# A four-layer image kernel: the order of the first loads and sums, and the last chunk and tail of a scan

## Chip, cores and metric

The kernel runs on one core of a Trainium2 chip. The metric is the device time in microseconds of one execution; before the change the median of three runs is 3623.33 us.

## What is computed

An input of 48 x 48 positions with 768 channels, float32, goes through four layers: an attention block, a spectral filter, a scan with a rotating state, and a second spectral filter. Two places of it matter here. The attention block begins with a layer norm and one product:

```python
xn = layernorm(x, ln1_g, ln1_b)
qkv = xn.reshape(B, H * W, C) @ qkv_w + qkv_b
```

The scan layer makes its inputs from one projection of x, then applies twelve steps and an output product:

```python
B_proj = silu(x @ W_B + b_B + B_bias)      # C_proj the same; Xb = silu(x @ W_X + b_X)
alpha = jax.nn.sigmoid(x @ W_dec + b_dec)  # gamma the same, from W_lam
theta = x @ W_th + b_th
for i in range(12):
    inj = _rope(B_base, theta * (i + 1)) * Xb
    Hst = diffuse(Hst)                     # a 3 x 3 convolution of each channel
    Hst = alpha * Hst + inj                # i = 0
    Hst = alpha * Hst + (1.0 - gamma) * alpha * prev + gamma * inj   # i > 0
    prev = inj
Hg = _rope(C_base, theta * 12) * Hst
return silu(Ho @ W_out + b_out)            # Ho is Hg with its axes turned
```

## The kernel before

Large products are done as 2 x 2 block products with seven terms instead of eight. So each needs sums of blocks of both operands, made on VectorE or GpSimd. The tile framework orders each engine's instructions by its own planner; an instruction pinned with `keep_in_program_order` keeps its place in the order of the program.

**Start of the attention block** (`qkv_phase`). Rows of x come in tiles of 128 x 768, three to a block, loaded on SP's queue by `load_x` (line 282), behind the loads of ln_g and ln_b (line 109). `prepare` normalises three tiles: statistics, a square root on ScalarE and small operations on VectorE (lines 73 to 88), scaling (line 89), then transposes on TensorE into PSUM (line 98) and evacuation with gain and bias, in turn on ScalarE and VectorE (lines 100, 102). The transposes use the pool `qkv_t` with two banks; the products of v use `qkv_m` with six. The weights of the first column block come as w[0], w[1], w[6] and a21 (lines 411 to 415). `combine` makes w[3], w[2], w[5], w[4] of them on GpSimd (lines 134 to 137). `sums` makes the same kind of sums of x on VectorE (lines 142 to 145), named t1, t2 and t4 here; the second of them overwrites a block of x. `rows_in_seven` (line 156) then runs the seven products of v in groups of nine matmuls, called v_0 to v_6. v_2 needs w[2] and t2. Partial results of v_0 are copied by ScalarE (line 172), those of v_1 and later added by VectorE (lines 174 to 180), and GpSimd adds the bias (line 299).

On SP's queue the store of all seven blocks of w to DRAM (line 431, 4 MB) stands early, ahead of most loads for the products of q and k (lines 348 to 350). The sums of those weights are GpSimd's too. `load_windows` (line 194) loads a table of relative positions on ScalarE's queue at the very start and copies it on VectorE; rm is its maximum (line 425), kb the scaled bias of k (line 423).

**Projection for the scan** (`scan_phase`). The projection (line 1186) runs in eight chunks q. After each, VectorE adds biases into za and g (line 1187), the angle is reduced (lines 1081 to 1087), ScalarE makes its sines (lines 1161, 1162), the SiLUs (line 1203) and the sigmoids (lines 1206, 1207); VectorE turns B (line 1380) and makes H (line 1216) and the states s0 and s1 (lines 1244 to 1250). In the last chunk several are pinned. Changing between groups of functions on ScalarE shows in the trace as a load of a table. ScalarE also spreads alpha (line 1263) and multiplies by gamma (line 1226).

**The scan** has eleven steps of eight groups of channels. TensorE does the convolution (line 1279) into four PSUM tiles of two banks, VectorE multiplies by alpha and adds the state (lines 1281, 1283), GpSimd prepares the next product t (line 1287), a tile of a ring of six, which ScalarE copies into PSUM (line 1288). GpSimd also turns C between steps, with c and cr tiles of the same ring (line 1380), and stores it to cr_d.

**The tail.** In the last step a group of turned C is loaded back as crg, two buffers (line 1291), and multiplied with H into the tile s0, by GpSimd for seven groups and by VectorE for the eighth (line 1305). When the scan's pools are closed, `turned` transposes the result on TensorE (line 1348) and ScalarE copies it into tiles hT of a new pool (line 1350), whose memory is that of the closed pools. The output products (line 1364), called so, follow, and with them the first products of the last layer, so_f (line 1495).

Of the kernel before, what the change touches and what calls it, by code (L numbers as in the profile page):

```python
# [12 lines left out]
F32 = mybir.dt.float32  # L13
# [7 lines left out]
P = 128  # L21
G = 48
# [16 lines left out]
NWR = KP * KTW  # L39
NBR = NWR + KP * 2 * KTH  # L40
SAFE = 64.0

NB, BS = 8, 96
KW = G // 2 + 1
# [48 lines left out]
def transpose_norm(nc, psum, xhs, xnT, ident, g, b, name):  # L93

    for cc in range(NC):
        ps = psum.tile([P, 512], F32, tag="t", name=f"{name}_tp{cc}")
        for t in range(3):
            nc.tensor.transpose(ps[:, t * P : (t + 1) * P], xhs[t][:, cc * P : (cc + 1) * P], ident)
        if cc % 2:
            nc.vector.tensor_scalar(xnT[:, cc, :], ps[:, :TB], g[:, cc : cc + 1], b[:, cc : cc + 1], ALU.mult, ALU.add)  # L100
        else:
            nc.scalar.activation(xnT[:, cc, :], ps[:, :TB], AF.Identity, bias=b[:, cc : cc + 1], scale=g[:, cc : cc + 1])


def load_cols(nc, pool, v, n, name):

    t = pool.tile([P, n], F32, tag=name, name=name)
    with nc.allow_non_contiguous_dma(reason="small vector"):
        nc.sync.dma_start(t, v.rearrange("(n p) -> p n", p=P))
    return t  # L110


# [19 lines left out]
def combine(eng, p, s1, s2, s3, s4):  # L132

    eng.tensor_tensor(s1, p[2], p[3], ALU.add)
    eng.tensor_tensor(s2, s1, p[0], ALU.subtract)
    eng.tensor_tensor(s3, p[0], p[2], ALU.subtract)
    eng.tensor_tensor(s4, p[1], s2, ALU.subtract)
# [56 lines left out]
def load_windows(nc, pool, relT):  # L194


    t = pool.tile([P, 2, 2 * G - 1, 2], F32, tag="windows", name="windows")
    rel = pool.tile([P, 2, 2 * G - 1], F32, tag="rel", name="rel")
    nc.vector.memset(t, 0.0)
    for s in range(2):  # L200
        rows = slice(s * HD, (s + 1) * HD)
        nc.scalar.dma_start(rel[rows], relT)
        nc.vector.tensor_copy(t[rows, :, :, s], rel[rows])
    return t

# [38 lines left out]
        yield  # L244


def qkv_phase(tc, ident, x, qkv_w, qkv_b, windows, ln_g, ln_b, q_d, k_d, v_d, rw_d, rh_d, wqk_d, wv_d, flag, home, ahead):

# [15 lines left out]
    with (  # L266
# [3 lines left out]
        ExitStack() as inner,  # L270
    ):
        kp, xp, wp = (inner.enter_context(tc.tile_pool(name=f"qkv_{n}", bufs=bufs, side="left")) for n, bufs in (("k", 1), ("x", 3), ("w", 3)))
        g = load_cols(nc, kp, ln_g, NC, "ln1_g")
        b = load_cols(nc, kp, ln_b, NC, "ln1_b")
        wv = qkv_w.rearrange("(c p) n -> p c n", p=P)
        Xs, ops = {}, {}

        def load_x(sb, half):
            for t in range(3):
                i = (2 * sb + half) * 3 + t  # L280
                Xs[i] = xp.tile([P, C], F32, tag="x", name=f"x_{i}", bufs=6)
                nc.sync.dma_start(Xs[i], x[i * P : (i + 1) * P, :])

        def prepare(sb, half):

            blk = 2 * sb + half
            if half == 0:
                ops[sb] = home.tile([P, NC * TS], F32, tag="xn", name=f"xnT_{sb}").rearrange("p (c n t) -> p c n t", c=NC, n=2)
            xhs = [layernorm_rows(nc, xp, Xs.pop(3 * blk + t), f"ln1_{blk}_{t}") for t in range(3)]
            transpose_norm(nc, pt, xhs, ops[sb][:, :, half, :], ident, g, b, f"n1_{blk}")  # L290

        def sums(sb):
            ts = (kp.tile([P, NC2, TB], F32, tag=f"x{n}", name=f"xn{n}_{sb}") for n in ("T1", "T2", "T4"))
# [112 lines left out]
        with tc.tile_pool(name="qkv_v0", bufs=1, side="right") as vp:  # L406
            w = vp.tile([P, 7, NC2, TB], F32, tag="wv", name="wv")
            a21 = vp.tile([P, NC2, TB], F32, tag="a21", name="a21")
            load_x(0, 0)
            for k in range(2):  # L410
                nc.sync.dma_start(w[:, k], wv[:, k * NC2 : (k + 1) * NC2, 2 * C : 2 * C + TB])
            prepare(0, 0)
            load_x(0, 1)
            nc.sync.dma_start(w[:, 6], wv[:, NC2:, 2 * C + TB :])
            nc.sync.dma_start(a21, wv[:, :NC2, 2 * C + TB :])
            vb = load_bcast(nc, kp, qkv_b[2 * C : 3 * C], C, "vb")
            qkb = load_cols(nc, kp, qkv_b[0 : 2 * C], 2 * NC, "qkb")
            kb = kp.tile([P, NC], F32, tag="kb", name="kb")
            qms, kms = (qp.tile([P, NC, NSB], F32, tag=n, name=n) for n in ("qms", "kms"))
            prepare(0, 1)  # L420
            combine(nc.gpsimd, (w[:, 0], w[:, 1], a21, w[:, 6]), w[:, 3], w[:, 2], w[:, 5], w[:, 4])
            sums(0)
            V.tensor_scalar(kb, qkb[:, NC : 2 * NC], HD**-0.5, None, ALU.mult)
            rm = qp.tile([P, 2], F32, tag="rm", name="rm")
            V.tensor_reduce(rm, windows.rearrange("p t k s -> p t (k s)"), axis=AX.X, op=ALU.max, apply_absolute_value=True)
            pz = qp.tile([P, 2, NC], F32, tag="pz", name="pz")
            V.memset(pz, 0.0)
            onec = qp.tile([P, 1], F32, tag="onec", name="onec")
            V.memset(onec, 1.0)
            v_rows(0, lambda n: w[:, n])  # L430
            nc.sync.dma_start(wv_d, w)

        with tc.tile_pool(name="qkv_o", bufs=1, side="right") as op:
# [94 lines left out]
            V.tensor_scalar(flag, mx, SAFE, None, ALU.is_lt)  # L528
            while steps or ready:
                advance()  # L530


def load_bias(nc, bt, p0, rw_d, rh_d, h, g, t0, n):
# [352 lines left out]
def mlp_phase(tc, ident, w1s_d, b1, w2, w2s_d, b2, ln_g, ln_b, xr_d, xa_d, follow_in):  # L886
# [8 lines left out]
    with (  # L895
# [18 lines left out]
        def prepare(sb, half):  # L914

            blk = 2 * sb + half
            if half == 0:
                ops[sb] = [cp.tile([P, NC, 2, TB], F32, tag="x2nT", name=f"x2nT_{sb}")]
                ops[sb] += [cp.tile([P, NC2, TB], F32, tag=f"x{n}", name=f"x{n}_{sb}") for n in ("T1", "T2", "T4")]
            xhs = []  # L920
            for t in range(3):
                xt = xp.tile([P, C], F32, tag="x", name=f"ml_x_{blk}_{t}", bufs=6)
                r0 = (3 * blk + t) * P
                nc.sync.dma_start(xt, xr_d[r0 : r0 + P, :])
                xhs.append(layernorm_rows(nc, xp, xt, f"ln2_{blk}_{t}"))
            X, t1, t2, t4 = ops[sb]
            transpose_norm(nc, pt, xhs, X[:, :, half, :], ident, g, b, f"n2_{blk}")
            if half:
                ops[sb] = block_sums(nc, X, t1, t2, t4)

# [162 lines left out]
def scan_phase(tc, ident, w, wts, rows_back, xh, x_close, c_d, cr_d, out_open):  # L1093
# [24 lines left out]
    with tc.tile_pool(name="sc_s", bufs=1, side="left") as sp:  # L1118
# [9 lines left out]
        with (  # L1128
# [15 lines left out]
            with (  # L1144
# [27 lines left out]
                for q in range(NQ):  # L1172
# [3 lines left out]
                    for t in range(R4):  # L1176
# [11 lines left out]
                        biased.pop(0)()  # L1188
                        if t < R4 - 1:
                            biased.pop(0)()  # L1190
                    g3 = g.rearrange("p (n r) t -> p n r t", r=RR)
                    c, x = za[:, :NCR, :], za[:, NA - 1 - RR : NA - 1, :]
                    thz = za[:, NCR + NN : NCR + NN + NM, :]
                    alq = al[:K, :, prs]
                    ga = temp([1, R4], "ga", q)
                    th = temp([NM * R4], "th", q)
                    V.tensor_copy(th, thz.rearrange("p m t -> p (m t)"))
                    cs = sincos(th, q, "t1")

                    pin = tc.keep_in_program_order if q == NQ - 1 else lambda ins: ins  # L1200
                    pin(biased.pop(0)())
                    for t in (x, g, c):
                        pin(nc.scalar.activation(t, t, AF.Silu))

                    V.tensor_tensor(g.rearrange("p (n r) t -> p n (r t)", r=RR), g.rearrange("p (n r) t -> p n (r t)", r=RR), x.rearrange("p r t -> p (r t)").unsqueeze(1).to_broadcast([K, NN, RR * R4]), ALU.mult)
                    pin(nc.scalar.activation(alq, za[:, NCR : NCR + NN, :], AF.Sigmoid))
# [46 lines left out]
            with (  # L1253
# [16 lines left out]
                def step(it, gr):  # L1270
# [13 lines left out]
                    if it + 1 < ITERS:  # L1284
                        t = tp.tile([P, GC, RR, NPR], F32, tag="t", name=f"t_{it}_{gr}")
                        m0 = (gr * GC) % NM
                        GP.tensor_tensor(t, sc[:, ch], c1[:, m0 : m0 + GC].unsqueeze(2).to_broadcast([P, GC, RR, NPR]), ALU.mult)  # L1287
                        nc.scalar.copy(pv, t.rearrange("p (b n) r t -> p b (n r t)", b=2))
                    else:
                        cr = tp.tile([P, NQ, GC * RR, R4], F32, tag="crg", name=f"crg_{gr}", bufs=2)  # L1290
                        nc.sync.dma_start(cr[:K], cr_d[:K, :, gr * GC * RR : (gr + 1) * GC * RR])
                        crs[gr] = cr

# [38 lines left out]
        with (  # L1332
# [7 lines left out]

            yield x3, psum
            hTs = {}

            def turned(j, q4):

                ps = pt.tile([P, 512], F32, tag="t", name=f"ht_{j}_{q4}")
                for t in range(4):
                    nc.tensor.transpose(ps[:, t * P : t * P + K], hg[:K, 4 * q4 + t, j * P : (j + 1) * P], ident[:K, :K])
                hTs[j, q4] = tp.tile([P, 4, 2, G], F32, tag=f"hT{j}_{q4}", name=f"hT_{j}_{q4}", bufs=1)
                nc.scalar.copy(hTs[j, q4], ps.rearrange("p (i s w) -> p i s w", i=4, s=2)[:, :, :, :G])  # L1350


# [31 lines left out]
def block_kernel(ctx: ExitStack, tc: tile.TileContext, a: dict):  # L1384
# [39 lines left out]
            loads[2](bts[g], (0, 0), g)  # L1424
        ahead.extend((loads, kvs, qbs, bts, ones, oneh))

    windows = load_windows(nc, atc, a["relT"])
    qkv_phase(tc, ident, x, a["qkv_w"], a["qkv_b"], windows, a["ln1_g"], a["ln1_b"], q_d, k_d, v_d, rw_d, rh_d, wqk_d, wv_d, flag, home, load_ahead)

    def opened(name, shape, side):  # L1430
        stack = ExitStack()
# [498 lines left out]
```

## Time and profile before

| | |
|---|---|
| runs before | 3623.33, 3620.8, 3623.38 us |
| profiled execution | 3626.7 us, its span 3624.9 us |
| mean granted TensorE clock | 0.987 |
| first TensorE instruction | 11.69 us |
| v_2 begins, TensorE then without a gap to 103 us | 41.25 us |
| last projection product of the scan ends | about 3019.7 us |
| first convolution product | 3030.59 us |
| last convolution product ends | about 3274.7 us |
| transposes resume | 3284.05 us |

All times are from the start of the span. A timeline row has the start, the duration, the engine, the line and the operation, what it writes and reads, and how many instructions are merged; in brackets stands the idle time of the engine before it and what ended it. POOL is GpSimd, DVE VectorE, ACT ScalarE, PE TensorE and PEld its weight loads. A float32 matmul has two records in this trace, a transpose one. Ends of matmuls are modelled.

### The profile page before, as it was taken

Reading aid. Unit: us, or ns where it says so; the run is one execution under the profiler, and the core shown is the slowest. Engines: PE = TensorE matmul, PEld = TensorE weight load, DVE = VectorE, ACT = ScalarE, POOL = GpSimd, SP = SyncE. Lnnn points to the kernel's source line nnn. Section 1 sums busy time; section 2 is a strip of 40 time slices with the busy share of each in tenths; the row PEclk is TensorE's granted clock in tenths of the full one; section 3 lists DMA queues with packets and bytes.
Section 4 is the critical chain, followed back from the end, with each engine's and each line's share of the span. In section 5 each row is a group of like instructions: output and inputs, shape, how many; then the busy total and the mean of one; then the engine's idle time right before and its main releaser. Section 6 shows DMA issues by size and latency. Waiting matters only on the chain.

```text
span 3624.9 us, 52111 instructions
## 1 busy us (share of the span) xinstructions
PE 3539.1 (98%) x20914; PEld 2174.5 (60%) x20914; DVE 2002.9 (55%) x3014; ACT 1138.5 (31%) x1731; POOL 685.8 (19%) x570
## 2 busy tenths in 40 slices
PE   7999999999999999999999999999999998999998
PEld 4666654444444444555555555555578777995685
DVE  6644456767676776564244324233145478994445
ACT  1222244444555554113101210120033365223341
POOL 4211101111111110340000000000023304961131
PEclk9999999999999999999999999999999999999999
DMA  7555555656545443443345334434444303113345
GB/s 248 205 194 173 197 163 164 185 143 157 162 121 151 125 125 86 125 152 125 107 136 174 106 106 140 146 109 123 140 131 105 94 21 104 33 30 101 95 113 157
DMA packets 257371, 477.66 MB, mean 132 GB/s; under 512 B 36031, under 2 KB 209919, under 8 KB 250913
## 3 DMA queue, kind: packets, MB, share of 16 engines
q1 hardware_dynamic: 247152, 453.20, 41.8%
q10 hardware_dynamic: 9968, 21.04, 1.6%
q8 instruction: 168, 2.75, 0.3%
q14 instruction: 83, 0.67, 0.1%
HBM read 330.53 MB, written 143.62 MB: 131 GB/s over the span
## 4 chain that ended last, share of the span: by engine, by line
PE 87%; DVE 4%; DMA 3%; POOL 3%; ACT 2%; issue 1%; SPq 0%; ACTq 0%; DVEq 0%; POOLq 0%
PE p L959 14%; PE p L1022 13%; PE s L623 12%; PE av L654 12%; PE qk L361 6%; PE c L1186 4%; PE v L169 3%; PE s L633 3%; PE pj L169 2%; PE f_z L1594 2%; PE f_z L1595 2%; PE f_x L1559 2%; PE so L1364 2%; PE f_u L1609 2%; POOL t L1287 2%
## 5 line engine op out<-in xcount | busy, mean ns | idle before, releaser
L643 DVE TENSOR_TENSOR acc<-acc,p 128x928 f32<-128x928 f32 (+1 forms) x480 | 560.5, 1168 | 264.1 <-ACT p L635 222.6
L635 ACT ACTIVATE p<-s 128x928 f32<-128x928 f32 (+1 forms) x540 | 505.9, 939 | 492.2 <-PE s L633 470.2
L623 PE MATMUL s<-qt,kv 64*128 64x464 f32 (+1 forms) x2160 | 521.9, 559 | 7.8 <-DMA qt<-q_d 5.7
L1022 PE MATMUL p<-w,h 128*128 128x384 f32 x1512 | 492.7, 486 | 0.0
L654 PE MATMUL av<-p,kv 128*64 128x464 f32 (+1 forms) x2160 | 443.0, 554 | 0.0
L1022 PEld LDWEIGHTS p<-w,h 128*128 128x128 f32 x1512 | 286.2, 190 | 196.9
L633 PE MATMUL s<-bt,oneh 64*128 64x464 f32 (+1 forms) x1080 | 400.9, 731 | 0.7 <-DMA bt<-rh_d 0.7
L654 PEld LDWEIGHTS av<-p,kv 128*64 128x64 f32 x2160 | 147.0, 137 | 262.0 <-issue 250.6
L623 PEld LDWEIGHTS s<-qt,kv 64*128 64x128 f32 x2160 | 203.1, 187 | 164.8 <-issue 153.6
L959 PE MATMUL p<-x2nT,w 128*128 128x384 f32 x864 | 292.7, 488 | 2.8 <-issue 2.8
L1279 PE MATMUL c<-H,bands 128*48 128x96 f32 x5632 | 243.8, 247 | 11.2 <-issue 10.9
L361 PE MATMUL qk<-xnT,wqk 128*128 128x384 f32 x756 | 249.8, 487 | 0.3 <-DMA wqk<-wqk_d 0.3
L1279 PEld LDWEIGHTS c<-H,bands 128*48 128x48 f32 x5632 | 234.5, 123 | 20.7 <-issue 11.3
L959 PEld LDWEIGHTS p<-x2nT,w 128*128 128x128 f32 x864 | 164.8, 191 | 118.3 <-issue 4.6
L959 PE MATMUL p<-xT,w 128*128 128x384 f32 x648 | 220.7, 486 | 0.0
L998 POOL TENSOR_TENSOR rr<-rr,ml_b 128x1152 f32<-128x1152 f32 x12 | 31.8, 2648 | 954.0 <-DMA rr<-xr_d 645.5
L361 PEld LDWEIGHTS qk<-xnT,wqk 128*128 128x128 f32 x756 | 141.4, 190 | 93.3 <-issue 0.9
L954 ACT ACTIVATE h<-h,ml_b 128x384 f32<-128x384 f32 x144 | 88.3, 614 | 345.8 <-DVE h L974 173.6
L1287 POOL TENSOR_TENSOR t<-s,c 128x768 f32<-128x768 f32 x80 | 144.5, 1830 | 182.7 <-DMA bands<-in_bands_dram 171.8
L959 PEld LDWEIGHTS p<-xT,w 128*128 128x128 f32 x648 | 123.1, 190 | 85.9
L633 PEld LDWEIGHTS s<-bt,oneh 64*128 64x128 f32 x1080 | 107.0, 188 | 105.6 <-issue 103.2
L169 PE MATMUL v<-wv,xnT 128*128 128x384 f32 x378 | 133.8, 499 | 0.6 <-DVE xnT L144 0.5
(326 smaller groups left out, 4665.5 us busy)
## 6 DMA issues: line engine op xcount, KB each, us to landing
w<-w1s_d SPq DMA_DIRECT2D x36, 768.0 KB, 4.1
w<-w2s_d SPq DMA_DIRECT2D x36, 768.0 KB, 4.4
w<-w1s_d SPq DMA_DIRECT2D x36, 576.0 KB, 3.7
w<-in_mlp_w_dram SPq DMA_DIRECT2D x27, 768.0 KB, 4.6
wqk<-wqk_d SPq DMA_DIRECT2D x12, 1344.0 KB, 10.9
yu<-f_ys SPq DMA_DIRECT2D x24, 672.0 KB, 3.8
f_yt<-yu SPq DMA_DIRECT2D x20, 720.0 KB, 6.6
yu<-f_us SPq DMA_DIRECT2D x18, 720.0 KB, 4.6
```

The costliest lines, as they stand in the source:

```text
L169: nc.tensor.matmul(p[:, :TB], lhsT=rhs[n][:, c, t * P : (t + 1) * P], rhs=w[:, c, :], start=c == 0, stop=c == NC2 - 1)
L361: nc.tensor.matmul(p[:, :TB], lhsT=w[:, n, c, :], rhs=ops[sb][n][:, c, :], start=c == 0, stop=c == NC2 - 1)
L623: nc.tensor.matmul(ps[:, s, :n], lhsT=keys[pr % 2][rows, kt * P : (kt + 1) * P], rhs=held(c)[rows, :n], start=True, stop=False)
L633: nc.tensor.matmul(ps[:, s, :n], lhsT=oneh[rows, b % 2, :], rhs=bts[b // 2][rows, j, :n], start=False, stop=True)
L635: nc.scalar.activation(p, ps[:, :, :n], AF.Exp)
L643: nc.vector.tensor_tensor(probs[c], probs[c], p, ALU.add)
L654: nc.tensor.matmul(avs[c][rows, : size(c)], lhsT=vals[pr % 2][:, kt, rows], rhs=p[:, s, :], start=kt == 0, stop=kt == NT - 1)
L959: nc.tensor.matmul(p[:, :TB], lhsT=w[n][:, c, :], rhs=rhs[n][:, c, :], start=c == 0, stop=c == NC2 - 1)
L1022: nc.tensor.matmul(ps[t][:, :TB], lhsT=hs[left, f][:, t * P : (t + 1) * P], rhs=wt[:, f % KW2, :], start=f == 0, stop=f == NF2 - 1)
L1186: nc.tensor.matmul(ps[:K, i, :n], lhsT=v[:, c, tok : tok + K], rhs=w[:, cc, c0 : c0 + n], start=cc == NC - 1, stop=cc == 0)
L1279: nc.tensor.matmul(ps[r0 : r0 + G, k // 4, cols], lhsT=bands[:, n - GC, i, :] if gr else bands0[:, n, i, :], rhs=H[:, n, :, d : d + NPR], ...
L1287: GP.tensor_tensor(t, sc[:, ch], c1[:, m0 : m0 + GC].unsqueeze(2).to_broadcast([P, GC, RR, NPR]), ALU.mult)
```

## The change

At the start: x_1 and ln_g, ln_b are loaded on ScalarE's queue, x_0 and x_2 first on SP's. Ten products of a zeroed tile, which nobody reads, stand ahead of TensorE's first transposes. The transposes of block 0 use the six banks of `qkv_m`. The four weight sums are VectorE's, between the sums of x, partly pinned. The position table is loaded on SP's queue after the first weights. By the planner's new order the 4 MB store of w comes after the loads of wqk_0, wqk_1 and part of wqk_2, and VectorE has both remaining weight sums and both remaining x sums ahead of the evacuation of v_1.

In the scan: the last chunk has the g addition and SiLUs ahead of the sines, crg tiles are of the ring of six, and the transposed result is copied into s1, which the last step has read.

```diff
 def load_x(sb, half):
-                nc.sync.dma_start(Xs[i], x[i * P : (i + 1) * P, :])
+                if i == 1:
+                    tc.keep_in_program_order(nc.scalar.dma_start(Xs[i], x[i * P : (i + 1) * P, :]))
+                else:
+                    nc.sync.dma_start(Xs[i], x[i * P : (i + 1) * P, :])
 def prepare(sb, half, meanwhile=lambda: None):
+            meanwhile()
+            pool, tag = (pm, "m") if blk == 0 else (pt, "t")
...
             load_x(0, 0)
+            g, b = (load_cols(nc, kp, v, NC, n, nc.scalar, tc) for n, v in (("ln1_g", ln_g), ("ln1_b", ln_b)))
+            warm = kp.tile([P, 3, TB], F32, tag="o", name="warm", bufs=2)[:, 0, :]
+            V.memset(warm, 0.0)
+            p = pm.tile([P, 512], F32, tag="m", name="warm_p")
+            for _ in range(WARM):
+                nc.tensor.matmul(p[:, :TB], lhsT=warm[:, :P], rhs=warm, start=True, stop=True)
             prepare(0, 0)
...
-            prepare(0, 1)
-            combine(nc.gpsimd, (w[:, 0], w[:, 1], a21, w[:, 6]), w[:, 3], w[:, 2], w[:, 5], w[:, 4])
-            sums(0)
+            def first_sums():
+                tc.keep_in_program_order(V.tensor_tensor(w[:, 3], a21, w[:, 6], ALU.add))
+                V.tensor_tensor(w[:, 2], w[:, 3], w[:, 0], ALU.subtract)
+
+            prepare(0, 1, first_sums)
+            V.tensor_tensor(t1, x12, x11, ALU.subtract)
+            V.tensor_tensor(t2, x22, t1, ALU.subtract)
+            tc.keep_in_program_order(V.tensor_tensor(w[:, 4], w[:, 1], w[:, 2], ALU.subtract))
+            tc.keep_in_program_order(V.tensor_tensor(w[:, 5], w[:, 0], a21, ALU.subtract))
+            V.tensor_tensor(x12, x22, x12, ALU.subtract)
+            V.tensor_tensor(t4, x21, t2, ALU.subtract)
+            windows = load_windows(nc, atc, relT)
...
+                    last = q == NQ - 1
+                    def silu():
+                        pin(biased.pop(0)())
+                        for t in (x, g, c):
+                            pin(nc.scalar.activation(t, t, AF.Silu))
+                    if last:
+                        silu()
                     V.tensor_copy(th, thz.rearrange("p m t -> p (m t)"))
                     cs = sincos(th, q, "t1")
-                    pin(biased.pop(0)())
-                    for t in (x, g, c):
-                        pin(nc.scalar.activation(t, t, AF.Silu))
+                    if not last:
+                        silu()
...
-                        cr = tp.tile([P, NQ, GC * RR, R4], F32, tag="crg", name=f"crg_{gr}", bufs=2)
+                        cr = tp.tile([P, NQ, GC * RR, R4], F32, tag="t", name=f"crg_{gr}")
...
+            free = s[1].rearrange("p n r t -> p (n r t)")
-                hTs[j, q4] = tp.tile([P, 4, 2, G], F32, tag=f"hT{j}_{q4}", name=f"hT_{j}_{q4}", bufs=1)
+                at = (j * (NPR // 4) + q4) * 4 * 2 * G
+                hTs[j, q4] = free[:, at : at + 4 * 2 * G].rearrange("p (i s w) -> p i s w", i=4, s=2)
                 nc.scalar.copy(hTs[j, q4], ps.rearrange("p (i s w) -> p i s w", i=4, s=2)[:, :, :, :G])
```

## The prediction

> **What bounds the kernel.** The page's busy row first: TensorE has work 98% of the span, so only the places where it does not, or runs slowly, can be won.
>
> ```profile
> PE 3539.1 (98%) x20914; PEld 2174.5 (60%) x20914; DVE 2002.9 (55%) x3014; ACT 1138.5 (31%) x1731; POOL 685.8 (19%) x570
> ```
>
> So I cut the edited stages into windows. Columns: window, length, then busy us (instructions) of PE, PEld, DVE, ACT, POOL, then granted clock, DMA share, GB/s.
>
> ```profile
> 0.00:10.00 10.00, 0.00 (x0) 0.00 (x0) 5.08 (x20) 1.69 (x3) 0.71 (x6) 1.00 0.72 217
> 10.00:20.00 10.00, 7.29 (x21) 4.65 (x22) 7.75 (x32) 2.30 (x5) 2.18 (x1) 1.00 0.92 306
> 20.00:30.00 10.00, 4.17 (x15) 2.48 (x14) 9.17 (x17) 1.15 (x4) 8.19 (x4) 0.85 0.62 209
> 30.00:40.00 10.00, 10.00 (x37) 6.08 (x36) 7.67 (x15) 2.39 (x4) 0.00 (x0) 0.81 0.84 361
> ...
> 3019.00:3031.00 12.00, 1.12 (x10) 0.69 (x10) 8.18 (x21) 8.62 (x15) 0.00 (x0) 0.70 0.78 271
> ...
> 3275.00:3285.00 10.00, 1.90 (x13) 1.73 (x14) 3.17 (x3) 0.86 (x2) 4.61 (x3) 0.74 0.30 76
> ```
>
> Three holes: the first 40 us (18.5 us idle, slow clock), the hand-over to the scan (10.9 us idle), the end of the scan (8.1 us idle). From 41.25 and from 3285.6 TensorE is busy almost without a gap for a long stretch, so a stage that starts earlier ends as much earlier. The timeline shows what ends each hole.
>
> ```profile
> 21.39 1.64 DVE L84 TENSOR_TENSOR ln_q<-ln_r 128x1 f32<-128x1 f32 x1
> 22.97 2.61 POOL L135 TENSOR_TENSOR wv<-wv 128x1152 f32<-128x1152 f32 x1
> 23.13 2.46 DVE L85 TENSOR_TENSOR ln_q<-ln_q,ln_ve 128x1 f32<-128x1 f32 x1
> 25.71 2.57 DVE L85 TENSOR_TENSOR ln_q<-ln_q,ln_ve 128x1 f32<-128x1 f32 x1
> 29.17 0.69 PE L98 MATMUL n_tp<-ident,x 128*128 128x128 f32 x2 [5.83 <-DVE x L89]
> ...
> 3023.06 1.28 ACT L1203 ACT_TABLE_LOAD   x1
> 3030.59 22.60 PE L1279 MATMUL c<-H,bands 128*48 128x96 f32 x494 [10.88 <-issue]
> ...
> 3281.93 1.48 DVE L1305 TENSOR_TENSOR s<-H,crg 112x768 f32<-112x768 f32 x1 [5.21 <-DMA crg<-cr_d]
> 3283.52 0.86 ACT L1350 COPY hT<-ht 128x384 f32<-128x384 f32 x2 [23.25 <-DVE s L1305]
> 3284.05 1.76 PE L1348 MATMUL ht<-ident,s 112*128 112x112 f32 x8 [6.22 <-ACT hT L1350]
> ```
>
> At the start a one-element VectorE sum takes 1.6 to 2.6 us: it ends when GpSimd's 2.6 us sum ends. That made TensorE wait 5.83 us. In the scan's tail a copy waits for the last product with crg, which waited for its DMA.
>
> **Part A, the start.** Rows of block 0: x_0 is issued at 0.74 instead of 1.83, with x_1 beside it on ScalarE's queue. I take the statistics 1.1 us earlier, from 5.3 (before 6.43). Then by the rows of before: six BN_STATS at about 0.47 and their small operations 3.4 us, the small operations of all three tiles 1.5, scales 0.6 each: ready at 10.85, 11.45, 12.15 (before 11.5, 12.1, 13.3). The window copies and rm (1 us of VectorE) leave this path and return later.
>
> Unread products: ten, from about 1.4, after a 0.4 us memset. Before, a product took 1.28 us at the slow clock and 0.65 at full. The trace's first products start at 11.69 and are still slow at 20: 8.7 us, though with gaps. By that row the ten end near 12, 1.1 us after the first tile is ready. The Trainium skill ("TensorE: Matmul & The Clock Gate", "What's actually happening") has the clock released after about 3.4 us of sustained work: 2.7 slow products and 7.3 fast ones, end at 9.7, no delay. The second start (29.17, fast from about 33.3) took 4.1 us, which is nearer, and ten products have no gaps: I take no delay, and keep 1.1 us for the range.
>
> Transposes of block 0 now have six PSUM banks; at full clock they take 0.11 each (six in 0.67), so the last tile's end about 13.0; the nine products of v_0 follow, 5.85 us. Block 1's rows are ready at about 18.5, 19.8, 20.5 (VectorE: 3 us of statistics after the evacuations end at 14.9, then scales), so v_0, v_1 and the transposes between fill TensorE to 27.3.
>
> VectorE meanwhile must do, from 20.5: two weight sums, three evacuations at 0.65, t1, one window copy, t2. A 128x1152 sum is 1.27 on VectorE (row L142) against 2.6 on GpSimd. Alone: v_2 could start at 27.7 (before 41.25). The pinned first weight sum waits for a; before it landed at 17.7, so that costs nothing. But behind t2 stand four more sums, the second copy and kb before the first evacuation of v_1, and v_3's first product needs that bank (v_1 and v_2 hold all six). Alone: 33.6, when v_2 ends. Before, v_3 began at 41.25 + 5.85 = 47.1. Gain alone: 13.5.
>
> It is not alone. wqk_0 and wqk_1 no longer sit behind the 4 MB store on SP, so GpSimd's eight sums of 128x384, 1.0 us each (before at 51 to 65), come as soon as wb lands. I estimate 23.6: a lands 1.1 us earlier (16.6), then 2.4 MB of vb, x and wqk at about 390 GB/s. Who waits for whom is seen in attention:
>
> ```profile
> 569.52 4.90 DVE L643 TENSOR_TENSOR acc<-acc,p 128x928 f32<-128x928 f32 x3 [2.04 <-ACT p L635]
> ...
> 569.70 1.89 POOL L136 TENSOR_TENSOR pw0p<-pw0p,pw0b 128x384 f32<-128x384 f32 x1
> ```
>
> The two take turns, one for one. Eight turns lie in the chain, some under evacuations from PSUM, which do not wait (L100 took its usual 0.68 at 20.80): 0.7 to 0.9 each. t2 is done at 29.3, the first v_1 evacuation at 40.1; v_3 starts at 40.1. Bounds: 13.5 (GpSimd late or never in the way) and 5, if TensorE's 4.9 us wait at v_3 also drops the clock. I take 47.1 - 40.1 = **7.0**, as GpSimd's work is issued early by the order. Next late is POOL's wqk_2, behind v_o and the moved 4 MB store; TensorE needs it near 90, some 25 us later than I expect it.
>
> At nothing, with their cover: the relT loads now on SP (0.6 each to issue) stand ahead of x for block 2, read after v_3; the three issues on ScalarE (to about 2.5) and its 1.28 us table load end before the first Sqrt near 7; w's first block, behind x in the queue, is read at 13 and was there at 15.07 before; kb and rm are read in q and k, after 60. Uncovered, each would cost its own 0.2 to 1.3 us.
>
> **Part B, hand-over.** All in the last chunk. The g addition now follows za's (3020.9). Before: Abs and two Sin, a load of 1.28, three SiLUs, a second load, sigmoids. Now the SiLU load runs while ScalarE is idle (4.69 us before 3022.32), SiLUs end at 3022.5, and the order shows no load between SiLU and Sin. The angle reduction with g*x in its middle (0.9) ends at 3023.6, sin at 3024.05; the turning starts at 3024.1, before 3026.32. Sigmoids come 1.7 earlier, before their reader. H, the u products and alr on ScalarE (one alr moved behind u_1) move likewise by 2.1, and so do c_d's store and GpSimd's first t (3039.45). The rule ("ScalarE: Activation LUTs", "What ACT_TABLE_LOAD costs") gives 2.66 a switch, which would make it 3.5; the row has 1.28 and the SiLU 0.01 after it. I take the row: **2.1** (1 to 2.5).
>
> **Part C, tail.** crg gets the ring of six: crg_0 to crg_5 are issued as ScalarE frees t tiles (3247 to 3260), crg_6 and 7 after GpSimd's first two products. At about 4 us each all land before use (last 3270). GpSimd's seven products at 1.88 then follow H: end 3276.1; VectorE's last, after H at 3276.7, at 3278.2. The first transposes still wait for that H (3276.88, as before), but their copies go into s1, free by then, and no longer wait for the end of every H read: first copy 3277.5 instead of 3283.52. From 3278.0, five groups of transposes at 0.4, twelve output products at 0.65: the first so_f at about 3288.7, before 3297.68. Before, 3279.8 to 3290 ran at half clock; now the gap is 2.3 us (3274.55 to 3276.88) and I take it as full. Gain **9.0**; 6 if the clock falls, 10 at best.
>
> **Sum.** 7.0 + 2.1 + 9.0 = 18.1. The profiled execution took 3626.7 (span 3624.9 and 1.8 around it), giving 3608.6; it lies 3.4 above the median 3623.33, so 3605.2 for the median.
>
> **Rivals.**
> 1. GpSimd does not meet the chain (wb lands after 33): A is 13.5, total 24.6, 3598.7. For: my landing is an estimate. Against: SP's order puts wqk early. 0.20.
> 2. The clock falls twice: the v_3 wait (4.9, where 3.65 us idle dropped it before) costs 2, the tail 3: total 13, 3610. For: half clock after both holes before. 0.22.
> 3. The unread products don't lift the clock: they run 12.8 us to 14.2, 3.3 late, and transposes run slowly, 1.9: A about 2, total 13, 3610. Against: after 33.3 steady products were fast. 0.05.
> 4. Slower: the pinned weight sum waits for a, and block 1's evacuations and so TensorE queue behind it. Each microsecond of landing after 20.5 costs one; with 18 to lose, the kernel is slower once a lands past 38.5, and at 50 by 11.5: 3635. Against: a landed at 17.7 from the same place in the queue. 0.03.
> My forecast: 0.50.
>
> Range 3597 to 3612: rivals 1 to 3 lie in it; the ends are A at 13.5 with C at 10, and A at 2 with B and C low. A change under 0.2% (7.2 us) is about what a measurement here cannot tell. Faster than that needs a gain over 7.2, which C alone nearly gives: 0.94; within 0.04; slower 0.02.
>
> **What would show it.** Right: statistics from about 5.3; full clock at the first transposes; L135 on wqk between 23 and 40, VectorE's sums stretched to 2.2; v_3 near 40; first scan product 2 us earlier against the projection's end; first so_f 9 us earlier against the scan's last product; no wait for crg. Wrong: v_3 before 36 (rival 1), a granted clock under 1 at 35 to 42 or in the tail (2), first transposes after 13 (3), VectorE waiting for a (4).

## The result and the profile after

The changed kernel takes 3601.79 us (median of 5 runs, 3599.88 to 3606.24), the kernel before 3623.33 beside it. The ratio is 0.9952 with a 95% interval of 0.9941 to 0.9962, a gain of 17.4 us (13.8 to 21.4); the two medians by themselves lie 21.5 apart. A second measurement of the same kernel gave 0.9948 (0.9935 to 0.9962). The profiled execution took 3605.15 us with a span of 3603.4, against 3626.7 and 3624.9: its span is 21.5 shorter.

The busy row still says 98% for TensorE, with the same 3539.1 us of work, so the whole gain is idle time and slow clock.

```profile
PE 3539.1 (98%) x20934; PEld 2173.6 (60%) x20934; DVE 2005.8 (56%) x3019; ACT 1140.3 (32%) x1731; POOL 679.0 (19%) x566
```

The edited stages again as windows of the changed kernel (window, length, busy us and count of PE, PEld, DVE, ACT, POOL, then granted clock, DMA share, GB/s). The last two are the hand-over to the scan and the scan's end, laid about 12 us earlier than in the rows of before.

```profile
0.00:10.00 10.00, 8.59 (x20) 4.66 (x20) 5.59 (x32) 1.89 (x4) 0.71 (x6) 1.00 0.84 258
10.00:20.00 10.00, 9.33 (x42) 5.98 (x42) 9.68 (x37) 3.54 (x9) 0.00 (x0) 1.00 1.05 336
20.00:30.00 10.00, 9.79 (x41) 5.81 (x40) 10.00 (x11) 2.02 (x3) 3.41 (x2) 1.00 0.90 245
30.00:40.00 10.00, 5.49 (x15) 2.92 (x14) 9.94 (x11) 0.00 (x0) 9.84 (x8) 0.80 0.57 241
40.00:50.00 10.00, 10.00 (x28) 5.74 (x27) 7.43 (x28) 0.61 (x3) 2.13 (x1) 0.86 0.90 358
3007.00:3019.00 12.00, 3.70 (x43) 3.27 (x43) 10.28 (x32) 9.54 (x18) 0.00 (x0) 0.72 0.96 348
3262.50:3272.50 10.00, 7.85 (x47) 5.50 (x44) 3.48 (x4) 4.24 (x8) 1.89 (x2) 0.83 0.48 117
```

TensorE is now busy from 1.4 to 33 with waits of at most 0.6 us, then has the one long hole that the forecast named, and the clock falls behind it (0.80, 0.86). The timeline of that place in the changed kernel shows VectorE and GpSimd in turns, each operation about 2.1 us, up to v_3 at 38.06:

```profile
26.07 1.36 DVE L441 TENSOR_TENSOR xnT<-xnT,xnT 128x1152 f32<-128x1152 f32 x1
26.59 1.69 POOL L137 TENSOR_TENSOR wqk<-wb,wqk 128x384 f32<-128x384 f32 x1 [25.28 <-DMA wb<-in_qkv_w_dram]
27.34 2.15 DVE L442 TENSOR_TENSOR wv<-wv 128x1152 f32<-128x1152 f32 x1
28.25 2.11 POOL L139 TENSOR_TENSOR wqk<-wqk,wb 128x384 f32<-128x384 f32 x1
29.42 2.15 DVE L443 TENSOR_TENSOR wv<-wv,a 128x1152 f32<-128x1152 f32 x1
...
35.73 0.94 DVE L206 COPY windows<-rel 64x190 f32<-64x190 f32 x1
38.06 2.29 PE L172 MATMUL v<-wv,xnT 128*128 128x384 f32 x3 [4.51 <-DVE v_o L181]
```

In the scan's tail of the changed kernel no row waits for crg. The first transposes still wait 2.15 us for H; the copy behind them now waits for the transposes alone:

```profile
3265.05 2.60 PE L1382 MATMUL ht<-ident,s 112*128 112x112 f32 x12 [2.15 <-DVE H L1316]
3266.11 0.48 ACT L1385 COPY s<-ht 128x384 f32<-128x384 f32 x1 [17.67 <-PE ht L1382]
3267.45 1.26 PE L1399 MATMUL so<-wo,s 128*96 128x384 f32 x2
```

To see where the 21.5 us went, I take the start of one product in both traces at each border; the gain between two borders belongs to the stage between them.

| stage | gain, us |
|---|---|
| start to first q and k product (70.3, 63.7) | 6.6 |
| to attention's first product | -0.2 |
| attention (1022.8, 1018.0) | 4.8 |
| projections, MLP, to the projection for the scan | 0.8 |
| hand-over and scan (255.2, 255.4) | -0.2 |
| tail to the last output product (107.4, 99.6) | 7.9 |
| rest | 1.8 |

The edits lie in the first, fifth and sixth stage, and these make 14.3 of 21.5. The hand-over is 2.6 us shorter up to the first scan product, and the scan has given it back by its last.

### The profile page after: what moved, and what is told of

The parts are those of the page before. It is cut to its first block, busy times and chain, and to the rows that moved or that the text cites. A ratio compares the mean times of both kernels' runs of the same rounds, so it can differ in the third digit from the quotient of the medians.

```text
span 3603.4 us, 52156 instructions
## 1 busy us (share of the span) xinstructions
PE 3539.1 (98%) x20934; PEld 2173.6 (60%) x20934; DVE 2005.8 (56%) x3019; ACT 1140.3 (32%) x1731; POOL 679.0 (19%) x566
```

## The experiments

**One table first.** Each run is the changed kernel with one edit; three columns are lengths in us in its trace (starts of products, as above: start to first q and k product; last product of the projection for the scan to last scan product; from there to the last output product), the last is its time against the kernel before on the same chip.

| run | start | hand-over, scan | tail | ratio (95%) |
|---|---|---|---|---|
| before | 70.3 | 255.2 | 107.4 | 1 |
| changed | 63.7 | 255.4 | 99.6 | 0.9952 (0.9941-0.9962) |
| again | 64.8 | 255.4 | 99.6 | 0.9948 (0.9935-0.9962) |
| start_old | 69.1 | 255.9 | 98.3 | 0.9969 (0.9958-0.9980) |
| scan_old | 58.5 | 255.0 | 99.6 | 0.9943 (0.9930-0.9957) |
| tail_old | 58.7 | 254.6 | 105.7 | 0.9968 (0.9956-0.9980) |
| clear | 57.6 | 254.6 | 99.6 | 0.9944 (0.9930-0.9958) |
| gp_late | 58.1 | 255.8 | 98.3 | 0.9942 (0.9928-0.9955) |
| warm0 | 58.5 | 255.6 | 98.3 | 0.9954 (0.9941-0.9968) |
| ring_old | 60.1 | 255.4 | 101.4 | 0.9954 (0.9940-0.9967) |
| band_late | 59.9 | 253.0 | 98.3 | 0.9937 (0.9924-0.9951) |
| tile_old | 58.8 | 255.5 | 101.1 | 0.9957 (0.9944-0.9971) |
| gp_mid | 60.7 | 255.3 | 98.3 | one run |
| best | 59.1 | 253.1 | 99.8 | 0.9950 (0.9936-0.9963) |

Single runs of one kernel spread over 3 to 11 us, so two ratios that differ by less than 0.2% are not told apart; the verdicts below rest on the lengths within a trace. The second column repeats best. The first has the two forms of the start that scan_old shows. The third has 98.3 and 99.6 for the same instructions: behind the same wait of 2.15 us for H the first transposes ran at full clock in some traces and at half clock in others (see Part C).

**start_old.** The hunks of the start are taken back, the others stay.

> The old start with the changed scan hand-over and tail. If the start is worth what the first q and k product shows (70.3 to 63.7), the time is 3608.4. Rival: the start also shifts GpSimd's weight sums against attention and so gave the 4 us more that the profile of the changed kernel shows between the start and the end of attention; then 3612 to 3613, and a wait of exp for a GpSimd sum with a TensorE hole of 2 us near 592 comes back in its trace. If that hole was an accident of the one execution of before, the trace of this run has no such hole.

Measured: 3611.62 us, ratio 0.9969; against the two ratios of the changed kernel that is about 7 us for the start. Its first q and k product is at 69.1. Attention took 1018.5 in this trace, as with the new start (1017.8 to 1020.5 in eleven traces, 1023.4 in one, band_late). So the 4.8 us in attention are not the start's. In the trace of before, exp stands still once for 3.00 us there, as its ScalarE row shows (TensorE idles 2.00 us and runs slowly for some us):

```profile
595.17 0.94 ACT L635 ACTIVATE p<-s 128x928 f32<-128x928 f32 x1 [3.00 <-POOL pw1p L136]
```

Three runs with the new start have the same wait of 3.0 us for pw1p (band_late, tile_old and gp_mid, whose attention took 1020.3 to 1023.4), the others 0.9 or nothing. So it belongs to the execution, and the rival falls. The stall is 3.9 of the 4.8 us; the other 0.9 came earlier in attention. In band_late it cost as much as before, with the clock at 0.60 behind TensorE's wait of 2.00 us; in tile_old and gp_mid 2.3 to 2.5, with the clock at full behind the same wait.

**scan_old.** The order of sines and SiLUs is taken back.

```
-                    if last:
-                        silu()
                     V.tensor_copy(th, thz.rearrange("p m t -> p (m t)"))
                     cs = sincos(th, q, "t1")
-                    if not last:
-                        silu()
+                    silu()
```

> The changed kernel with the old order in the scan's last chunk (sines, then SiLUs); start and tail stay changed. Theory 'given back': the 2.1 us of the hand-over are lost again in the scan's first groups, where GpSimd waits 2.56 us for sc to land and TensorE waits 1.34 and 0.92 for the sums behind it; then the time stays at 3601.8, within 1 us, and the first scan product lies 10.9 us behind the projection's last product instead of 8.3 while the last scan product moves by less than 0.5. Theory 'kept': that wait for sc belongs to the one profiled execution; then the time is 3603.9.

Measured: 3599.78, ratio 0.9943, no slower than with the new order. The first scan product lies 11.3 us behind the projection's last (new order 8.7 in every trace), and the last one at 255.0 (new 254.6 to 255.9). "Given back" stands by these lengths; the time alone cannot say it, as the start was 5.2 us shorter in this trace. What its trace showed by the way was the start: the same instructions up to 3000 us, and v_3 at 35.20 with the clock at full speed.

```profile
25.38 1.00 POOL L137 TENSOR_TENSOR wqk<-wb,wqk 128x384 f32<-128x384 f32 x1 [24.07 <-DMA wb<-in_qkv_w_dram]
25.78 0.71 DVE L206 COPY windows<-rel 64x190 f32<-64x190 f32 x1
26.34 7.35 POOL L139 TENSOR_TENSOR wqk<-wqk,wb 128x384 f32<-128x384 f32 x1
26.41 1.34 DVE L441 TENSOR_TENSOR xnT<-xnT,xnT 128x1152 f32<-128x1152 f32 x1
27.68 1.34 DVE L442 TENSOR_TENSOR wv<-wv 128x1152 f32<-128x1152 f32 x1
...
35.20 5.11 PE L172 MATMUL v<-wv,xnT 128*128 128x384 f32 x15 [1.31 <-DVE v_o L181]
```

GpSimd's sum (row L139) lasts 7.35 us in the trace against 1.00 alone, while five VectorE sums pass in 1.34 each; I read it as standing until they are through. The two do not take turns here.

**tail_old.** crg back in two buffers, the turned states back in tiles of their own.

> The changed kernel with the old tail: crg in its own two buffers and the turned states in tiles of their own. If the tail is worth what the trace shows up to the first output product and at the hand-over after it (7.9 and 1.4), the time is 3611.1, and the wait for crg and the 6 us wait of the transposes come back. If only the part up to the last output product is the tail's, it is 3609.7. If the clock at the tail was the larger part, 3607 or less.

Measured: 3607.97, ratio 0.9968, 6.5 us behind the mean of the changed kernel's ratios; its tail is 6.1 longer (105.7 against 99.6). The trace shows both old waits again: the copies until the last product with crg, the transposes for the copies.

```profile
3259.42 1.73 PE L1381 MATMUL ht<-ident,s 112*128 112x112 f32 x8 [2.15 <-DVE H L1316]
3265.53 0.86 ACT L1383 COPY hT<-ht 128x384 f32<-128x384 f32 x2 [22.72 <-DVE s L1338]
3266.07 1.76 PE L1381 MATMUL ht<-ident,s 112*128 112x112 f32 x8 [4.92 <-ACT hT L1383]
```

The other 1.8 of the 7.9 is in the execution of before: its wait there was 6.22, which is 1.3 of it.

**ring_old** and **tile_old**, the tail's two parts apart. The first undoes `tag="t"` of crg, the second the tile:

```
-                hTs[j, q4] = free[:, at : at + 4 * 2 * G].rearrange("p (i s w) -> p i s w", i=4, s=2)
+                hTs[j, q4] = tp.tile([P, 4, 2, G], F32, tag=f"hT{j}_{q4}", name=f"hT_{j}_{q4}", bufs=1)
```

> The changed kernel with only crg put back into its two buffers; the turned states stay in s1. If the tail's gain needs both parts, the last products wait for crg again, but the first transposes' copies do not wait for them: the first output product 5 us behind the last scan product as in the changed kernel, later groups then wait for the products with crg; I expect half of the 6 to 8 us, 3605. If the free tile alone makes the gain: 3602. If the ring alone: 3609.

> The changed kernel with only the turned states put back into tiles of their own, crg in the ring of six. With crg alone put back the last product for the output lay 101.3 us behind the last scan product (changed 98.3 to 99.5, both undone 105.7), so the free tile alone makes 4.4 of 6.2. If the two parts are complements, this run loses nearly all: the copies of the turned states wait for the last product with crg as before, 104 to 105, 3607. If the ring alone is the remaining 2 to 4: 102 to 103, 3604.

Measured: 3602.98 and 3605.93 (0.9954 and 0.9957); tails of 101.4 and 101.1. Each part alone brings 4.3 to 4.6 of 6.1 us, so they overlap, and my word "complements" was wrong. (In tile_old the first transposes ran at full clock, in tail_old at half, so up to 1.2 of the 4.6 can be the clock; the two still add up to more than 6.1.) With the ring alone (tile_old) crg lands in time, the last product with crg is early, and the copies wait little for it, holding TensorE 1.14; with the tile alone (ring_old) they do not wait for it at all, but VectorE's last product still waits 5.17 us for crg and also holds TensorE 1.14.

**clear.** The evacuations of v_1 stand ahead of the four sums that only v_4 to v_6 read; these, the window copies, kb and rm go one by one behind later evacuations (`then()` issues the next of them after each tile from v_1's last on).

```
-            tc.keep_in_program_order(V.tensor_tensor(w[:, 4], w[:, 1], w[:, 2], ALU.subtract))
...
-            v_rows(0, lambda n: w[:, n])
+            v_rows(0, lambda n: w[:, n], then)
```

> The changed kernel with the evacuations of v_1 put ahead of the four sums that only v_4 to v_6 need, and the window copies, kb and rm put later still. My theory, that the 4.5 us wait at v_3 and the half clock after it come from what stands before the first evacuation of v_1 on VectorE: v_3 starts at 33.3, right behind v_2, the clock stays full from 11 on, and the gain is 4.75 plus 2.3, so 3594.8. Rival: GpSimd's turns stretch the moved sums so that v_4 waits for its weight sum instead; then v_3 at 33.3 but a new wait near 39, and 3598 to 3601. Rival: the clock falls anyway; 3597.

Measured: 3599.26 (ratio 0.9944; its profiled execution 3596.13). The wait at v_3 is gone (v_3 at 34.41 rather than 33.3) and the clock is full, so what stood before the evacuation did make it; the first q and k product is at 57.6, with 0.91 us lost at v_2, since t2 took its turn with GpSimd (2.12 us). The start is 6.1 us shorter than in the trace on record and 0.9 or more shorter than in the traces without turns; the expected 3594.8 is not shown, as the ratio does not tell them apart.

**gp_late.** GpSimd's eight early sums wait for v_1's output, VectorE's order is untouched (the gate is a copy of two elements of that output).

```
...
+                    if pr < 2:
+                        nc.gpsimd.tensor_copy(w[:, 3:6:2, 0, 0:1], gate[0][:, 1:3, 0:1])
                     combine(nc.gpsimd, (w[:, 0], w[:, 1], wb, w[:, 6]), w[:, 3], w[:, 2], w[:, 5], w[:, 4])
```

> The changed kernel with GpSimd's sums of wqk_0 and wqk_1 made to wait for v_1's finished output (a copy of two elements of it into a sum that is overwritten later); VectorE's order up to there is unchanged. So far one trace of this start has VectorE and GpSimd taking turns (v_3 at 38.1, half clock after it, first q and k product at 63.7), two others have a single GpSimd sum of 7.35 us that waits while VectorE runs five operations at 1.34 (v_3 at 35.2, 58.6). If the shared path is the cause of both, it is out of the way here: every VectorE sum at 1.3, the window copy at 0.24, kb at 0.1, v_3 at 33.4 behind v_2 without a wait, no clock dip, first q and k product near 57, and a time of about 3599 with no run above 3603. If the chain on VectorE alone made the wait, v_3 stays at 35.

Measured: 3598.84 (3596.35 to 3601.07, ratio 0.9942). Its timeline has no gap in TensorE at all behind 26.10, the second window copy 0.26 (0.94 beside GpSimd) and kb 0.17 (0.85):

```profile
26.10 16.33 PE L172 MATMUL v<-wv,xnT 128*128 128x384 f32 x49
27.12 0.24 DVE L206 COPY windows<-rel 64x190 f32<-64x190 f32 x1
33.77 0.26 DVE L206 COPY windows<-rel 64x190 f32<-64x190 f32 x1
34.06 0.17 DVE L452 TENSOR_SCALAR kb<-qkb 128x6 f32<-128x6 f32 x1
```

From the start of t2 to the end of v_1's first evacuation VectorE takes 7.4 us here, 8.7 in scan_old and 11.9 in the changed kernel. So what VectorE shares with GpSimd is the cause of the wait in both forms. v_3 was at 34.74 and not 33.4, the product at 58.1 and not 57, for a reason outside the theory: ln_b, third on ScalarE's queue, landed late, and TensorE waited 1.27 us behind it. ring_old's timeline shows it largest:

```profile
14.01 1.79 ACT L103 ACTIVATE xnT<-n_tp,ln_b,ln_g 128x384 f32<-128x384 f32 x3 [5.19 <-DMA ln_b<-in_ln_b_dram]
14.73 1.56 PE L172 MATMUL v<-wv,xnT 128*128 128x384 f32 x4 [1.84 <-ACT xnT L103]
```

**gp_mid.** The same gate, but on t2 (the edit is shown against gp_late), so that GpSimd arrives inside VectorE's run.

```
-                        nc.gpsimd.tensor_copy(w[:, 3:6:2, 0, 0:1], gate[0][:, 1:3, 0:1])
+                        nc.gpsimd.tensor_copy(w[:, 3:6:2, 0, 0:1], ops[0][2][:, 0:2, 0:1])
```

> The changed kernel with GpSimd's sums of wqk_0 and wqk_1 held until t2 is done, so that they arrive while VectorE is already in its run of four more sums. In the trace with turns GpSimd's first sum came 0.5 us into a VectorE sum; in the five others a short VectorE copy stood there. If arriving inside a run of long sums makes the two take turns, this trace shows each VectorE sum behind t2 at 2.1 us, v_3 at 37 to 38 and a clock under 1 at 40. If GpSimd always loses against a run of VectorE sums, they take 1.34, its first waits 4 to 6 us, v_3 at 34.5 to 35.5 and the clock stays full. Only the stretch up to v_3 is compared: GpSimd's later order changes too.

Measured (one run, 3601.37): v_3 at 35.70, between the two figures, after a wait of 2.11 us, the clock 0.83 at 30 to 40.

```profile
27.38 1.35 DVE L444 TENSOR_TENSOR wv<-wv 128x1152 f32<-128x1152 f32 x1
27.53 2.52 POOL L358 COPY wqk<-xnT 128x2 f32<-128x2 f32 x2 [26.22 <-DVE xnT L443]
28.65 1.35 DVE L445 TENSOR_TENSOR wv<-wv,a 128x1152 f32<-128x1152 f32 x1
29.92 1.35 DVE L446 TENSOR_TENSOR xnT<-xnT 128x1152 f32<-128x1152 f32 x1
30.01 2.11 POOL L137 TENSOR_TENSOR wqk<-wb,wqk 128x384 f32<-128x384 f32 x1
31.19 2.15 DVE L447 TENSOR_TENSOR xnT<-xnT,xnT 128x1152 f32<-128x1152 f32 x1
```

Read as turns it fits: the two short copies (2.52 us for both) end about where a VectorE sum ends, the first long GpSimd sum stretches the VectorE sum that starts within it to 2.15. The gate itself used up two turns, which I had not counted. GpSimd does get in when it arrives inside the run; it did not in the six traces where its second sum came 0.07 to 0.08 us before t2's. Yet in clear a second sum 0.09 us ahead of t2's went first (0.99 us, t2 stretched to 2.12), so the order of the two starts does not settle it.

**warm0.** `WARM = 0`.

> The changed kernel without the ten unread products (it computes the same). If they matter as the trace says (3.9 us at half speed, then full), the transposes of block 0 begin at 10.6 at half speed, end near 15 instead of 13.1, VectorE's evacuations and all behind them come 2 us later, and the first q and k product lies 2 to 3 us later than in the changed kernel in the same mode of the port (60.6 to 61.6 against 58.6): 3604. If the wait for VectorE and the second weights hides it, the first q and k product moves by less than 0.5 and the time stays.

Measured: 3603.2, ratio 0.9954. The transposes take 4.17 us instead of 2.48 and v_0 begins at 14.44 instead of 12.9, as expected; at v_3 nothing of it is left.

```profile
10.47 4.17 PE L99 MATMUL n_tp<-ident,x 128*128 128x128 f32 x18 [10.47 <-DVE x L90]
14.44 4.30 PE L172 MATMUL v<-wv,xnT 128*128 128x384 f32 x12
...
35.22 5.11 PE L172 MATMUL v<-wv,xnT 128*128 128x384 f32 x15 [0.86 <-DVE v_o L181]
```

The first q and k product is at 58.5, as in scan_old. VectorE's chain to v_3 hides the unread products' gain; in this form of the start they are worth nothing.

**band_late.** The last of the seven band loads goes behind the first sc.

```
-                    if gr:
+                    if 0 < gr < NG - 1:
...
+                    if i == 2:
+                        nc.sync.dma_start(bands[:, NN - 2 * GC :], bands_d[:, NN - GC :])
```

> The changed kernel with the last of the seven band loads (768 KB) issued behind the first sc instead of ahead of it. The scan's hand-over gains 2.6 us at its first product in every trace of the new order, and loses 2.2 to 3.4 by its last, because sc lands 7.0 to 8.4 us after its issue instead of 5.5 (three bands stand between the stores and sc, before two) and GpSimd waits for it 1.9 to 3.3 us. If the band ahead of it is the cause: sc lands in about 5.6, no GpSimd wait over 0.5, no TensorE wait in the scan's first 40 us, the last scan product 246.2 behind the first (changed 248.3 to 249.7), and the kernel is 2 to 3 us faster than the changed one, 3599. If the order of GpSimd's work is the cause, the wait for the sums (1.3 and 0.9) stays and so does the time.

First two rows of scan_old, which has the old order of the last chunk (two bands behind the store of t, as before), then the timeline of the changed kernel, then that of band_late: SP's issues (a row of several begins with its first), GpSimd's first turning step, TensorE's waits:

```profile
3015.16 0.33 SPq L1246 DMA_DIRECT2D c_d<-t  x1
3015.53 0.93 SPq L1288 DMA_DIRECT2D bands<-in_bands_dram  x2
```

```profile
3020.34 0.33 SPq L1253 DMA_DIRECT2D c_d<-t  x1
3020.71 1.39 SPq L1295 DMA_DIRECT2D bands<-in_bands_dram  x3
3024.80 19.77 SPq L1347 DMA_DIRECT2D sc<-c_d  x3
3032.59 0.93 POOL L1415 TENSOR_TENSOR m<-c,sc 112x384 f32<-112x384 f32 x1 [2.56 <-DMA sc<-c_d]
3038.07 5.57 PE L1312 MATMUL c<-H,bands 128*48 128x96 f32 x128 [1.34 <-DVE s L1332]
3044.56 5.62 PE L1312 MATMUL c<-H,bands 128*48 128x96 f32 x128 [0.92 <-DVE s L1332]
```

```profile
3018.81 0.33 SPq L1253 DMA_DIRECT2D c_d<-t  x1
3019.18 0.93 SPq L1295 DMA_DIRECT2D bands<-in_bands_dram  x2
3023.27 0.43 SPq L1347 DMA_DIRECT2D sc<-c_d  x1
3023.75 0.43 SPq L1361 DMA_DIRECT2D bands<-in_bands_dram  x1
3028.68 0.92 POOL L1417 TENSOR_TENSOR m<-c,sc 112x384 f32<-112x384 f32 x1 [0.18 <-DMA sc<-c_d]
```

GpSimd starts on sc 5.4 us after its issue instead of 7.8, its wait falls from 2.56 to 0.18, the two waits of TensorE are gone, and hand-over and scan take 253.0 instead of 255.4: the new order now keeps 2.2 of its 2.6 us. The time, 3598.15 (ratio 0.9937), is the lowest of all, though its interval overlaps that of the changed kernel.

**again** and **best**. The changed kernel once more; and gp_late with band_late and with ln_g and ln_b issued ahead of x_1.

> The changed kernel itself, once more. Of six traces of this start, one has VectorE and GpSimd taking turns from 27.3 on (v_3 at 38.1, half clock, 5 us lost), five have GpSimd's second sum waiting 7.35 us while VectorE runs on (v_3 at 35.2 to 36.8). If that is a property of the single execution and not of the kernel, this trace shows one of the two: first q and k product at 63.7 or at 58.5 to 60.1, and single times that fall into two groups, near 3600 and near 3605.5. In the scan sc is late again and 2 to 3 us are lost.

> The changed kernel with three edits: GpSimd's first weight sums behind v_1's output (as in the run with v_3 at 34.6 and no wait), the last band behind sc (2.4 to 3 us), and ln_g and ln_b issued ahead of x on ScalarE's queue, since in three of seven traces ln_b landed at 13.4 to 13.9 and the first evacuation waited 1.2 to 1.9 us for it. If the three add: first q and k product at 56.5 to 57, the last scan product 246.3 behind the first, and 3595 to 3596. If the two small loads ahead of x only move the lateness to x: statistics of the second tile after 6.7, q and k product at 58, and 3597.

Measured: again 3602.98, with turns (v_3 at 38.84, first q and k product 64.8), and the same 255.4 for hand-over and scan. The single times, 3600.31 to 3603.74, do not fall into two groups, though: turns cost 5 us in the start, but other accidents of that size cover it. Best took 3601.48 (0.9950): the scan's 2.3 us are there (253.1), but the statistics of the second tile began at 8.60 instead of about 6.2, since x_1 now came late, and the start was 59.1: the third edit only moved the lateness. By the traces gp_late with band_late, without this third edit, should be the best; that was not run, and no version here is shown to beat the changed kernel by its time.

## Why the prediction was right

The median lies 3.4 us under the forecast of 3605.2, well in the range; by the ratio it would be 3605.9. But not all terms were right, and what made up for them was luck of the execution.

- **Part A** (7.0, traced 6.6): right in kind and, in that trace, by its mechanism: GpSimd's row of turns (lines 137 to 140 of the changed kernel), VectorE's sums at 2.15, v_3 near 40 (38.06). wb landed at 26.6 rather than 23.6 (2.4 MB at 390 GB/s behind 16.6 give 22.8, too), so t2 escaped, and six turns lay in the chain instead of eight. The gain at v_3 was 9.0 rather than 7.0, but the clock then fell after the 4.51 us wait, which I had kept as a bound: from v_3 to the first q and k product it took 25.6 us, 23.3 in scan_old. Failed is the assumption that turns are what always happens. In six of the eight traces of this start (all but the changed kernel's and again's: scan_old, tail_old, warm0, ring_old, band_late, tile_old) GpSimd stood behind VectorE's run, v_3 came at 35.2 to 36.8, and the first q and k product at 58.5 to 60.1: a gain of 10 to 12 us over before's 70.3. That is close to rival 1's 13.5 by another way: GpSimd was there, and lost.
- **Unread products**: they end at 9.99, as forecast (9.7), and lift the clock; the rows of the trace say 3.9 us of slow products, between the 3.4 and the 4.1 that the prediction weighs. But warm0 shows no gain from it at v_3. The forecast never asked what they are worth behind VectorE's chain.
- **At nothing**: the three loads on ScalarE's queue were not free: their issues were covered, but not the landing of ln_b. It came late in three of eleven traces that have x_1 ahead of it (gp_late, band_late, ring_old), and TensorE waited 1.2 to 1.8 us.
- **Part B** (2.1, traced -0.2): the step "so do c_d's store and GpSimd's first t" failed. The first scan product did come 2.6 us earlier, between the 2.1 of the row and the 3.5 of the rule for a table switch, nearer to the row. But with za's store issued earlier, one 768 KB band load changed sides of the store of t on SP's queue, and three instead of two bands stood ahead of c and sc. From the first scan product to the last it then took 245.9 to 247.2 instead of 243.7 to 243.9. I had the order of both kernels and read it by engines, not what is ahead of each load.
- **Part C** (9.0 at the first so_f; traced 7.3 there, 7.9 at the last output product): right in kind. The mis-sized term is the clock: I took the 2.15 us gap as harmless, and the window after it is at 0.83, with twelve transposes in 2.60 us where 0.11 each makes 1.3. But this, too, is luck of the execution. In five traces with the same tail (start_old, gp_late, warm0, band_late, gp_mid) the same wait left the clock at full, and so_f began 14.5 us behind the last scan product instead of 15.7: 8.5 of the 9.0, with 1.2 us for the clock. Of the rest, 0.2 is a slip of mine (so_f began at 3297.52 before, not 3297.68). From gp_late, beside tail_old's row of 1.73 above:

```profile
3259.96 0.96 PE L1386 MATMUL ht<-ident,s 112*128 112x112 f32 x8 [2.15 <-DVE H L1320]
```

- **What came on top**: 7.2 us of the 21.5 are in stages that no edit touches, 3.9 of them the stall of exp in the execution of before. By its three terms alone the trace would have given 3626.7 - 14.3 = 3612.4, where the forecast put 3608.6. That the median still comes out near the forecast fits the six traces in eight whose start gains 3.6 to 5.2 us more than the one on record; the single times are too wide apart to show it.
- Rival 2 (the clock falls twice) happened as described, at 2.3 and 1.2 us instead of 2 and 3. Rival 4 did not: VectorE's pinned sum began at 20.32, right behind the last scale.

## What to carry to other kernels

When a step moves earlier, write down for each load behind it what is ahead of it in its queue, before and after: one transfer that changes sides can eat the whole gain, out of sight of the place that was edited. Where two engines share a path, cost the chain both ways, in turns and with one engine standing, and prefer a dependency that keeps them apart. And take an end-to-end difference apart at fixed products: what lies in untouched stages may belong to the execution and not to the change, as here, where a run without the edits of the start had none of attention's loss.

## What the runs showed of the hardware

- VectorE and GpSimd on the same kind of sums have two forms of sharing with the same instructions: turns (2 of 8 traces), or GpSimd's 128x384 sum standing 7.35 us while five VectorE operations pass. In the six, GpSimd's second sum had been issued 0.07 to 0.08 us ahead of t2's; in the two, a GpSimd sum came 0.5 and 0.9 us into t2's. In clear a second GpSimd sum 0.09 us ahead of t2's was not kept out. The Trainium skill ("SBUF — State Buffer", "Who interferes with whom") has whichever is issued first hold the path for its whole instruction while the other blocks fully. For a pair of instructions the turns agree; a run of five VectorE operations that keeps out a GpSimd sum issued ahead of them does not, and there the measurement decides. What picks the form is not shown.
- Short operations wait as well: a 128x2 copy on GpSimd took about 1.3 us (two of them 2.52 in gp_mid, 0.31 in gp_late), kb (128x6) 0.85 instead of 0.17.
- The length of TensorE's wait alone did not tell whether the clock fell. It fell after 4.51 and 4.50 (the changed kernel, again) and after 2.11 us (gp_mid), and not after 1.31 (scan_old). Behind the tail's 2.15 the first transposes ran at half clock in six of 14 traces and at full in eight; behind attention's 2.00 it fell in two of four; and 3.07 in best left it full (18 transposes in 2.49 us). The skill ("TensorE: Matmul & The Clock Gate", "HAM oscillation") warns of gaps of over about 3.4 us; here shorter ones were enough in some executions. What decides it is not shown.
- In the first microseconds of the program products run at half speed while the granted clock row says 1.00 (warm0: 18 transposes in 4.17 us at 10.47); only the durations tell it.
